# A graph layer that sums 140 quads of edges in its loop, and the 141st in a branch at the end

## The chip, the core and the metric

The kernel runs on one core of a Trainium2 chip. A core has five engines, each with an instruction queue of its own: TensorE (PE, matrix products; its weight loads are listed as PEld), VectorE (DVE), ScalarE (ACT), GpSimd (POOL) and SyncE (SP), which here only starts transfers. [...]a "q" behind an engine's name (POOLq, SPq) means its sequencer, which handles branches, register loads, semaphores and the starting of transfers. Transfers run on 16 DMA engines. The metric is the device time of one execution in microseconds (us).

## The reference

The input is a graph of 12,500 nodes with 128 features each and 400,000 edges sorted by their target `dst`. Each edge has a length (`edge_weight`). With the biases written out:

```python
rbf = exp(-(distances[:, None] - centers) ** 2 / (2.0 * width * width))       # 50 centers, 0 to 10
cut = 0.5 * (cos(pi * distances / CUTOFF) + 1.0) * (distances <= CUTOFF)      # CUTOFF = 10
W = (silu(rbf @ fw1 + fb1) @ fw2 + fb2) * cut[:, None]
messages = (h[src] @ pw + pb) * W
agg = segment_sum(messages, dst, num_segments=num_atoms)
y = h + (silu(agg @ mw1 + mb1) @ mw2 + mb2)
out = layernorm(x + y)                                                        # h is x
```

An edge whose length is over 10 adds nothing to `agg`. The lengths are spread evenly from 0 to 56.3, so most edges drop out; in the inputs of the reference 71,145 of the 400,000 stay.

## The kernel before, in words

**Packing.** The edges are read in 7 chunks, 128 rows of consecutive edges at a time. `pack` moves the edges that stay to the front of each row, and an indirect store writes them densely, one after the other, to `packed` in device memory. What follows works on that dense list. 512 places of the list are a *quad*, two quads (one pass of `basis`, `first`, `silu`) an *oct*. `QB` says at which quad each chunk's share begins; its last entry, 141, is the number of quads for which there is room, and `NQ = QB[-1]` that of the quads that the loop works on. 141 quads have 72,192 places.

**The loop over quads** (L1043) does for each quad `q`: `fetch` (L638, four indirect gathers on POOL, 128 rows of 512 bytes each, into one of four buffers `quad` from quad 32 on); `radials` (lengths of an oct, spread over 64 partitions, one transfer a quad on SP); `basis` (ACT), `first` (PE) and `silu` (ACT) for the radial filter; `second` (PE, L707 and L710); `message` (DVE, L717: filter times gathered rows); `place` (DVE, four operations at L726 that build a 128x128 matrix of places and weights each); `sum_up` (PE, L742); `base_of` (DVE's queue loads the target column into a register) and `add` (DVE, L765, two operations that add the sums to `aggT`). Gathers are issued several quads ahead. `added(q)` says up to which quad the adds are done when quad `q` begins: in pairs up to `NQ - 14`, one quad behind after that. The order on every engine is the order in which the program issues the instructions; a small model of time (`clock`, `pool`, `there_at`) decides only where steps of `pack` and the gathers are put.

**Node groups.** `aggT` holds the sums, features on partitions. A group is 512 nodes and is named by its first tile of 128 nodes: 0, 4, ..., 96 (the last has 212 nodes). Since the edges are sorted, the first groups are complete long before the last quad. `begin` (L888) computes from `added`, `done_to` and `NQ` during which four quads a group is worked on: `node_first` (PE, L776 and L777, then tanh on ACT, L779), `node_silu` (DVE, L786), `node_second` (PE, L274 and L277), `node_stats` (DVE, L801 and L805). Every four groups `scaled` computes the scales of the normalization in 18 small DVE operations (L814 to L829), and `normalize` (ACT, L844) with its store follows, one group a quad. With 141 quads, group 76 is worked on in quads 131 to 134, group 80 in 133 to 136, group 84 in 136 to 139, and group 88 begins in quad 139 (`node_first`) and quad 140 (`node_silu`): it is the list `last`. Groups 92 and 96 are in no quad.

**The end.** After the loop the last quad is added (L1093), and `finish` (L860) works on group 88 from `node_second` on and on groups 92 and 96 from the start, then normalizes them; the halves of that last step are on ACT (L844) and DVE (L841).

**The check of the counts.** The kernel takes for granted that the edges fit into the room and the windows that it gives them. When all chunks are packed, `count` (L926) sums what would speak against it into one number, `bad_i`, and every engine loads that number into a register (L1092). At the end a branch (L1099) that runs if it is over 0 computes everything again in a general way. That branch isn't taken with these inputs; each engine jumps over it.

Of the kernel before, what the change touches and what calls it, by code (L numbers as in the profile page):

```python
# [10 lines left out]
F32 = mybir.dt.float32  # L11
BF16 = mybir.dt.bfloat16
I32 = mybir.dt.int32
# [6 lines left out]
P = 128  # L20
# [10 lines left out]

ROWS = (180, 435, 500, 512, 512, 512, 474)
CAPS = (58, 124, 136, 136, 136, 136, 132)
QB = (0, 7, 26, 48, 70, 93, 115, 141)
NC_ = len(QB) - 1
WIDE_C = 4
NQ = QB[-1]
AHEAD = 3  # L40
AHEAD_X = 4
FROM_X = 8
# [15 lines left out]
def kernel(  # L58
# [39 lines left out]
    E = src.shape[0]  # L98
    R_MAX = max(ROWS)
    NT = -(-N // P)  # L100
    NP = 2 * NQ
    MW = 2 * (NQ * QE + QE)

    CLEAR = (0, 128 * P, 384 * P, MW)
    assert H == P == W and GOT == LATER[1] + 4 and LATER[0] % GOT == 0
# [131 lines left out]
    def sides():  # L237


        nc.vector.tensor_scalar(third, part_f, -1.0, 1.0 / 3, op0=OP.add, op1=OP.mult)  # L240
        for v in (1.5, -1.5):
            nc.vector.tensor_scalar(third, third, v * (1 << 23), None, op0=OP.add)
        nc.vector.scalar_tensor_tensor(side, third, -3.0, part_f, op0=OP.mult, op1=OP.add)
        nc.vector.tensor_scalar(side, side, float(MW), None, op0=OP.mult)


        nc.vector.tensor_scalar(end, part_f, 2.0, float(2 * NQ * QE), op0=OP.mult, op1=OP.add)

    k_f, rbf_scale, rbf_bias = (keep.tile([P, 1], F32, name=k)
                                for k in ("k_f", "rbf_scale", "rbf_bias"))  # L250
# [34 lines left out]
    cnt = keep.tile([P, NC_], F32, name="cnt")  # L285
    span = keep.tile([P, NC_], F32, name="span")
    run = keep.tile([P, 1], F32, name="run")
    bad_i = keep.tile([1, 1], I32, name="bad_i")
    late_f = keep.tile([P, NC_], F32, name="late_f")
    nc.vector.memset(late_f, 0.0)  # L290
    lim = keep.tile([64, NC_], F32, name="lim")
# [355 lines left out]

    def quads(o):

        return [q for q in (2 * o, 2 * o + 1) if q < NQ]  # L650

    def radial(o, lengths, eng=None):

# [103 lines left out]
    def added(q):  # L757

        return max((q - 2) // 2 * 2 if q < NQ - 14 else q - 1, 0)
# [165 lines left out]

    def count():  # L926

        miss = keep.tile([P, 5], F32, name="miss")
        nc.vector.tensor_reduce(miss[:, 0:1], cnt, AX.X, OP.add)
        nc.vector.tensor_reduce(miss[:, 1:2], took, AX.X, OP.add)  # L930
        nc.vector.tensor_add(miss[:, 0:1], miss[:, 0:1], miss[:, 1:2])
        nc.vector.tensor_reduce(miss[:, 1:2], span, AX.X, OP.max)
        nc.vector.tensor_scalar(miss[:, 1:2], miss[:, 1:2], 127.5, None, op0=OP.is_gt)
        nc.vector.tensor_reduce(miss[:, 2:3], late_f, AX.X, OP.min)
        nc.vector.tensor_scalar(miss[:, 2:3], miss[:, 2:3], 0.0, None, op0=OP.is_lt)
        nc.vector.tensor_reduce(miss[:, 3:4], low, AX.X, OP.min)
# [106 lines left out]
    for q in range(NQ):  # L1043
# [44 lines left out]
        if not todo and not counted:  # L1088
            counted.append(q)
            count()  # L1090
        elif counted and total is None:
            total = nc.values_load(bad_i[0:1, 0:1], min_val=0, max_val=2 * E)  # L1092
# [6 lines left out]
    with tc.If(total > 0):  # L1099
        nc.vector.memset(aggT, 0.0)  # L1100
        def again(e0, seen):

            def column(ap, dt, name):
                t = work.tile([P, QT], dt, name=name, bufs=1)
                nc.sync.dma_start(t, ap[ds(e0, QE)].rearrange("(j p) -> p j", p=P))
                return t

            idx = column(src, I32, "idx")
            loc_i = column(dst, I32, "loc_i")
            lengths = column(edge_weight, F32, "lengths")  # L1110
            loc = work.tile([P, QT], F32, name="loc", bufs=1)
            nc.vector.tensor_copy(loc, loc_i)
            wgt = work.tile([P, QT], F32, name="wgt", bufs=1)
            near = work.tile([P, QT], F32, name="near", bufs=1)
            nc.vector.tensor_scalar(near, lengths, CUTOFF, 0.5, op0=OP.is_le, op1=OP.mult)
            if seen:
                nc.vector.memset(near[:, :seen], 0.0)
            fold(wgt, lengths, work.tile([P, QT], F32, name="fold_f", bufs=1),
                 work.tile([P, QT], I32, name="fold_i", bufs=1))
            cosine(wgt)  # L1120
            nc.vector.scalar_tensor_tensor(wgt, wgt, 1.0, near, op0=OP.add, op1=OP.mult)
            fetch(-2, idx)
            radial(-1, [edge_weight[ds(e0, QE)].rearrange("(o e) -> o e", o=1)])
            basis(-1)
            first(-1)
            silu(-1)
            second(-2)
            u = own(0, "msg", 0)
            for j in range(QT):
                nc.vector.tensor_scalar(u[:, j, :], pu_of[-2][:, j * H:(j + 1) * H],  # L1130
                                        wgt[:, j:j + 1], None, op0=OP.mult)
            free.append(pu_of.pop(-2))
            msg = own(1, "msg", 0)
            nc.vector.tensor_mul(msg, u, got_of.pop(-2))
            for n0 in range(0, N, WS):
                n = min(WS, N - n0)
                at = work.tile([P, QT], F32, name="at")
                nc.vector.tensor_scalar(at, loc, float(-n0), None, op0=OP.add)
                pa = bank()
                for j in range(QT):  # L1140
                    hot = work.tile([P, WS], F32, name="hot_all", tag="d", bufs=3)
                    nc.vector.tensor_scalar(hot[:, :n], iota_n[:, :n], at[:, j:j + 1],
                                            None, op0=OP.is_equal)
                    nc.tensor.matmul(pa[:, :n], msg[:, j, :], hot[:, :n],
                                     start=(j == 0), stop=(j == QT - 1))
                nc.vector.tensor_add(aggT[:, n0:n0 + n], aggT[:, n0:n0 + n], pa[:, :n])
                free.append(pa)

        with tc.For_i(0, E // QE, 1) as g:
            again(g * QE, 0)  # L1150
        if E % QE:
            again(E - QE, QT - E % QE // P)
        finish(tiles)


# [24 lines left out]
```

## Time and profile before

| | |
|---|---|
| median of 3 runs | 816.37 us (815.54 to 817.31) |
| the profiled execution: its own time | 819.14 us |
| the profiled execution: span, first to last instruction | 817.3 us |
| mean granted TensorE clock | 0.851 |
| POOL busy | 569.8 us (70%) |
| PE busy | 604.2 us (74%) |
| DVE busy | 587.5 us (72%) |
| ACT busy | 381.1 us (47%) |

The span is what the trace holds; the execution's own time is measured around it and is 1.84 us longer. In lines of instructions the columns are: start and duration in us (timeline), engine, line of the program, operation, result and sources by the program's names with their shapes, how many instructions, and in brackets how long the engine stood idle before them and what ended that. In lines that begin with a line number the columns after the bar are busy time in us, mean duration in ns, and idle time with what ended most of it; or, in lines with two slashed triples, minimum, median and maximum duration in ns and the start of the first and the last. "issue" is idle time in which the profile shows nothing that was waited for.

### The profile page before, as it was taken

What the parts mean: (1) busy time and instruction counts of PE and PEld (TensorE: products, weight loads), DVE (VectorE), ACT (ScalarE), POOL (GpSimd) and SP (SyncE); (2) the same over time, 40 slices, a digit from 0 to 9 for tenths busy, and PEclk for the clock granted to TensorE, in tenths of its full rate; (3) what the DMA queues carried; (4) which work ended last, traced back from release to release, by engine and by line L of the source; (5) the groups of instructions that cost most, each with busy time, mean ns of one, the idle gap of its engine ahead of it and who ended that gap; (6) DMA issues with size and microseconds to landing.
All of it is one profiled execution on the core that took longest, in us unless ns stands there. A gap on an engine that the chain in (4) does not pass through costs nothing.

```text
span 817.3 us, 11550 instructions
## 1 busy us (share of the span) xinstructions
PE 604.2 (74%) x3492; PEld 475.7 (58%) x3492; DVE 587.5 (72%) x1785; ACT 381.1 (47%) x536; POOL 569.8 (70%) x585
## 2 busy tenths in 40 slices
PE   6777878768776777866588678887777887688661
PEld 5766657547664555655456556665555665566551
DVE  7962568989978877979796677657566565756764
ACT  6536656434644353253354254636444633454421
POOL 1375477777777777777777777777777777777730
PEclk9978899977987776778779788999889989889875
DMA  6968734342234223332531622723622642371221
GB/s 198 263 201 246 191 85 105 90 117 75 74 107 112 65 65 112 103 78 53 144 87 52 164 65 79 194 68 104 170 79 58 159 122 78 80 188 52 81 83 48
DMA packets 88189, 91.86 MB, mean 112 GB/s; under 512 B 13864, under 2 KB 67832, under 8 KB 88120
## 3 DMA queue, kind: packets, MB, share of 16 engines
q1 hardware_dynamic: 69320, 52.77, 22.6%
q0 software_dynamic: 18544, 38.17, 18.6%
q8 instruction: 29, 0.48, 0.2%
q14 instruction: 40, 0.33, 0.1%
q10 hardware_dynamic: 256, 0.11, 0.1%
HBM read 75.29 MB, written 15.71 MB: 111 GB/s over the span
## 4 chain that ended last, share of the span: by engine, by line
DVE 24%; POOL 20%; DMA 20%; issue 16%; PE 14%; ACT 3%; DVEq 2%; SPq 0%; POOLq 0%; ACTq 0%
POOL quad L643 20%; DMA quad<-proj,srci 18%; DVE hot L726 4%; PE sums L742 4%; PE bank L277 3%; DVE aggT L765 3%; DVE quad L726 2%; PE bank L710 2%; DVE msg L717 2%; DVEq L751 2%; PE ph L693 2%; DVE quad L717 1%; DVE r_d L438 1%; DVE nodes L429 1%; PE bank L595 1%
## 5 line engine op out<-in xcount | busy, mean ns | idle before, releaser
L643 POOL DMA_INDIRECT quad<-proj,srci x532 | 524.9, 987 | 169.6 <-issue 131.7
L710 PEld LDWEIGHTS bank<-fw_sb,s 128*128 128x128 f32 x1128 | 175.2, 222 | 37.1 <-issue 28.8
L710 PE MATMUL bank<-fw_sb,s 128*128 128x128 f32 x1128 | 173.5, 304 | 0.0
L699 ACT ACTIVATE s<-ph 128x1024 f32<-128x1024 f32 (+1 forms) x71 | 72.3, 1018 | 197.9 <-PE ph L693 197.8
L742 PEld LDWEIGHTS sums<-hot,msg 128*128 128x128 f32 x696 | 92.3, 206 | 115.4 <-DVE msg L717 84.8
L742 PE MATMUL sums<-hot,msg 128*128 128x128 f32 x696 | 109.3, 304 | 52.6 <-DVE msg L717 52.5
L742 PE MATMUL sums<-quad,quad 128*128 128x128 f32 x432 | 79.3, 342 | 67.8 <-DVE quad L717 67.6
L742 PEld LDWEIGHTS sums<-quad,quad 128*128 128x128 f32 x432 | 70.2, 247 | 74.3 <-DVE quad L717 74.3
L717 DVE TENSOR_TENSOR msg<-bank,quad 128x512 f32<-128x512 f32 x87 | 59.6, 685 | 71.9 <-DMA quad<-proj,srci 62.7
L726 DVE TENSOR_SCALAR hot<-iota_n,dl,cut 128x128 f32<-128x128 f32 x348 | 98.6, 358 | 12.7 <-PE sums L742 8.9
L693 PE MATMUL ph<-rbf,w_sb 51*128 51x512 f32 x282 | 89.5, 711 | 1.5 <-ACT s L699 1.4
L717 DVE TENSOR_TENSOR quad<-bank,quad 128x512 f32<-128x512 f32 x54 | 37.1, 688 | 56.1 <-DMA quad<-proj,srci 54.3
L765 DVE TENSOR_TENSOR aggT<-aggT,sums 128x128 f32 x212 | 60.4, 285 | 22.3 <-PE sums L742 10.9
L707 PE MATMUL bank<-fb_b,ones_b 96*128 96x512 bf16 x141 | 61.5, 436 | 19.3 <-DVE msg L717 8.7
L683 ACT ACTIVATE rbf<-d,rbf_bias,rbf_scale 128x512 f32<-128x512 f32 (+1 forms) x71 | 57.0, 803 | 37.9 <-DMA d<-near_d 37.7
L726 DVE TENSOR_SCALAR quad<-iota_n,dl,cut 128x128 f32<-128x128 f32 x216 | 61.8, 360 | 3.0 <-issue 0.7
L779 ACT ACTIVATE zt<-bank 128x512 f32<-128x512 f32 (+1 forms) x25 | 14.6, 583 | 81.5 <-PE bank L777 81.5
L844 ACT ACTIVATE x<-x,by,rs 128x128 f32<-128x128 f32 x91 | 37.1, 481 | 30.6 <-DVE by L814 30.6
L277 PEld LDWEIGHTS bank<-pw_sb,xT 128*128 128x128 f32 x260 | 40.0, 222 | 11.3 <-issue 5.1
L684 ACT ACT_TABLE_LOAD x36 | 46.2, 1283 | 0.6
L699 ACT ACT_TABLE_LOAD x36 | 46.2, 1283 | 0.6
L684 ACT ACTIVATE rbf<-rbf 128x512 f32<-128x512 f32 (+1 forms) x71 | 44.7, 630 | 1.5
(169 smaller groups left out, 744.2 us busy)
## 6 DMA issues: line engine op xcount, KB each, us to landing
d<-near_d SPq DMA_DIRECT2D x141, 128.0 KB
x<-in_x_dram SPq DMA_DIRECT2D x48, 256.0 KB
quad<-proj,srci POOLq DMA_INDIRECT x532, 2.6
proj<-hp SPq DMA_DIRECT2D x24, 256.0 KB
out_dram<-x SPq DMA_DIRECT2D x24, 256.0 KB
packed<-zero_i SPq DMA_DIRECT2D x6, 188.0 KB
pair<-packed SPq DMA_DIRECT2D x3, 264.0 KB
r_d<-in_edge_weight_dram SPq DMA_DIRECT2D x3, 256.0 KB
```

Source lines behind the costliest of these rows:

```text
L277: nc.tensor.matmul(to[:m, k, :], lT[:, k * P:k * P + m], w, start=False, stop=(k == a + c - 1))
L643: nc.gpsimd.indirect_dma_start(out=got[:, j, :], out_offset=None, in_=proj if table is None else table, in_offset=bass.IndirectOffsetOnAxi ...
L683: nc.scalar.activation(rbf[:u], d[:u], AF.Square, bias=rbf_bias[:u], scale=rbf_scale[:u])
L684: nc.scalar.activation(rbf[:u], rbf[:u], AF.Exp, scale=-1.0 / (2.0 * width * width))
L693: nc.tensor.matmul(ph[:, h, :], w1_sb[p0:p0 + KR], rbf[p0:p0 + KR], start=True, stop=True)
L699: nc.scalar.activation(s[:, :n], ph[:, :n], AF.Silu)
L707: nc.tensor.matmul(pu, ones_b[:, :P], bias_b["fb2"].rearrange("k j f -> k (j f)"), start=True, stop=False)
L710: nc.tensor.matmul(pu[:, j * H:(j + 1) * H], s[:, j * P:(j + 1) * P], fw2_sb, start=False, stop=(j == QT - 1))
L717: nc.vector.tensor_mul(msg, pu.rearrange("p (j f) -> p j f", j=QT), got_of.pop(q))
L726: nc.vector.tensor_scalar(hot[:, j, :], iota_n[:, :W], dl[:, at[0], at[1]], cut[:, at[0], at[1]], op0=OP.is_equal, op1=OP.mult)
L742: nc.tensor.matmul(pa[:, k * W:(k + 1) * W], msg[:, j, :], hot[:, j, :], start=(j % n == 0), stop=(j % n == n - 1))
L765: nc.vector.tensor_add(to, to, pa[:, k * W:(k + 1) * W])
```

## The change

`NQ` becomes 140, while the room for packed edges stays at 141 quads (`NP`, `MW` and the end of the packed list are now computed from `QB[-1]`). The loop so works on quads 0 to 139. Everything that is computed from `NQ` follows: `added` changes its rule at quad 126 instead of 127, group 76 is worked on in quads 130 to 133, groups 80 and 84 keep their quads, group 88 is in no quad any more and belongs to `finish` with 92 and 96, and the x rows of these three groups are loaded in quad 136.

`count` computes two more numbers: by how many the staying edges exceed 140 x 512 = 71,680 (0 if they don't), and the sum of that and the number from before. All three are loaded into registers on every engine. At the end an outer branch (`either > 0`) holds two inner ones: `more > 0` works on quad 140 and on groups 92 and 96 again, with the functions of the loop, and `total > 0` is the branch from before, unchanged. With 71,145 edges all three numbers are 0.

```diff
-NQ = QB[-1]
+NQ = QB[-1] - 1
...
-    NP = 2 * NQ
-    MW = 2 * (NQ * QE + QE)
+    NP = 2 * QB[-1]
+    MW = 2 * (QB[-1] * QE + QE)
...
-        nc.vector.tensor_scalar(end, part_f, 2.0, float(2 * NQ * QE), op0=OP.mult, op1=OP.add)
+        nc.vector.tensor_scalar(end, part_f, 2.0, float(2 * QB[-1] * QE), op0=OP.mult, op1=OP.add)
...
-    bad_i = keep.tile([1, 1], I32, name="bad_i")
+    bad_i = keep.tile([1, 3], I32, name="bad_i")
...
-        return [q for q in (2 * o, 2 * o + 1) if q < NQ]
+        return [q for q in (2 * o, 2 * o + 1) if q < QB[-1]]
...
-        miss = keep.tile([P, 5], F32, name="miss")
+        miss = keep.tile([P, 6], F32, name="miss")
         nc.vector.tensor_reduce(miss[:, 0:1], cnt, AX.X, OP.add)
+        nc.vector.tensor_copy(miss[:, 4:5], miss[:, 0:1])
...
-        nc.tensor.matmul(cp[:1, :4], ones[:, 0:1], miss[:, :4], start=True, stop=True)
-        nc.vector.tensor_reduce(miss[0:1, 4:5], cp[:1, :4], AX.X, OP.add)
+        nc.tensor.matmul(cp[:1, :5], ones[:, 0:1], miss[:, :5], start=True, stop=True)
+        nc.vector.tensor_reduce(miss[0:1, 5:6], cp[:1, :4], AX.X, OP.add)
+        nc.vector.tensor_copy(bad_i[:, 0:1], miss[0:1, 5:6])
+        nc.vector.tensor_scalar(miss[0:1, 5:6], cp[:1, 4:5], float(-NQ * QE), 0.0, op0=OP.add,
+                                op1=OP.max)
         free.append(cp)
-        nc.vector.tensor_copy(bad_i, miss[0:1, 4:5])
+        nc.vector.tensor_copy(bad_i[:, 1:2], miss[0:1, 5:6])
+        nc.vector.tensor_add(bad_i[:, 2:3], bad_i[:, 0:1], bad_i[:, 1:2])
...
             total = nc.values_load(bad_i[0:1, 0:1], min_val=0, max_val=2 * E)
+            more = nc.values_load(bad_i[0:1, 1:2], min_val=0, max_val=E)
+            either = nc.values_load(bad_i[0:1, 2:3], min_val=0, max_val=3 * E)
...
-    with tc.If(total > 0):
-        nc.vector.memset(aggT, 0.0)
+    with tc.If(either > 0):
+
+        with tc.If(more > 0):
+            o = NQ // 2
+            fetch(NQ)
+            radial(o, [near_d[2 * NQ:2 * NQ + 2].rearrange("(o p) e -> o (p e)", o=1)])
+            basis(o)
+            first(o)
+            silu(o)
+            second(NQ)
+            place(NQ)
+            sum_up(NQ, message(NQ))
+            base_of(NQ)
+            add(NQ)
+            finish([t0 for t0 in tiles if (t0 + 4) * P > done_to(2 * NQ)])
+
+
+        with tc.If(total > 0):
+            nc.vector.memset(aggT, 0.0)
...
```

More of the change, by code (lines that the diff above doesn't have):

```diff
@@ L1096 @@
     finish([t0 for t0 in tiles if t0 not in begin], last)
-    with tc.If(total > 0):
-        nc.vector.memset(aggT, 0.0)
[L1101 to L1139, printed above, removed]
-                for j in range(QT):
[L1141 to L1153, printed above, removed]
@@ new lines, with again, column @@
+    with tc.If(either > 0):
[14 more added lines that the diff above has]
+            nc.vector.memset(aggT, 0.0)
+            def again(e0, seen):
+                def column(ap, dt, name):
+                    t = work.tile([P, QT], dt, name=name, bufs=1)
+                    nc.sync.dma_start(t, ap[ds(e0, QE)].rearrange("(j p) -> p j", p=P))
+                    return t
+                idx = column(src, I32, "idx")
+                loc_i = column(dst, I32, "loc_i")
+                lengths = column(edge_weight, F32, "lengths")
+                loc = work.tile([P, QT], F32, name="loc", bufs=1)
+                nc.vector.tensor_copy(loc, loc_i)
+                wgt = work.tile([P, QT], F32, name="wgt", bufs=1)
+                near = work.tile([P, QT], F32, name="near", bufs=1)
+                nc.vector.tensor_scalar(near, lengths, CUTOFF, 0.5, op0=OP.is_le, op1=OP.mult)
+                if seen:
+                    nc.vector.memset(near[:, :seen], 0.0)
+                fold(wgt, lengths, work.tile([P, QT], F32, name="fold_f", bufs=1),
+                     work.tile([P, QT], I32, name="fold_i", bufs=1))
+                cosine(wgt)
+                nc.vector.scalar_tensor_tensor(wgt, wgt, 1.0, near, op0=OP.add, op1=OP.mult)
+                fetch(-2, idx)
+                radial(-1, [edge_weight[ds(e0, QE)].rearrange("(o e) -> o e", o=1)])
+                basis(-1)
+                first(-1)
+                silu(-1)
+                second(-2)
+                u = own(0, "msg", 0)
+                for j in range(QT):
+                    nc.vector.tensor_scalar(u[:, j, :], pu_of[-2][:, j * H:(j + 1) * H],
+                                            wgt[:, j:j + 1], None, op0=OP.mult)
+                free.append(pu_of.pop(-2))
+                msg = own(1, "msg", 0)
+                nc.vector.tensor_mul(msg, u, got_of.pop(-2))
+                for n0 in range(0, N, WS):
+                    n = min(WS, N - n0)
+                    at = work.tile([P, QT], F32, name="at")
+                    nc.vector.tensor_scalar(at, loc, float(-n0), None, op0=OP.add)
+                    pa = bank()
+                    for j in range(QT):
+                        hot = work.tile([P, WS], F32, name="hot_all", tag="d", bufs=3)
+                        nc.vector.tensor_scalar(hot[:, :n], iota_n[:, :n], at[:, j:j + 1],
+                                                None, op0=OP.is_equal)
+                        nc.tensor.matmul(pa[:, :n], msg[:, j, :], hot[:, :n],
+                                         start=(j == 0), stop=(j == QT - 1))
+                    nc.vector.tensor_add(aggT[:, n0:n0 + n], aggT[:, n0:n0 + n], pa[:, :n])
+                    free.append(pa)
+            with tc.For_i(0, E // QE, 1) as g:
+                again(g * QE, 0)
+            if E % QE:
+                again(E - QE, QT - E % QE // P)
+            finish(tiles)
```

## The prediction

> **What bounds the kernel now.** I read the page first, then the order of time on POOL, then the last 40 us on all engines, then the releasers of the final branch. The costliest group is POOL's gathers, four for each quad of 512 edges:
>
> ```profile
> L643 POOL DMA_INDIRECT quad<-proj,srci x532 | 524.9, 987 | 169.6 <-issue 131.7
> L1092 POOLq TENSOR_LOAD <-bad_i x1: 505/505/505, 501.7 to 501.7; - x1
> L1099 POOLq COMPARE_BRANCH  x1: 54/54/54, 777.1 to 777.1; - x1
> L1099 SPq COMPARE_BRANCH  x1: 53/53/53, 812.2 to 812.2; - x1
> L1099 SPq EVENT_SEMAPHORE  x8: 17/17/17, 815.1 to 815.6; - x8
> ```
>
> From 91.2 us to 785.5 us POOL runs one gather after the other: 0.94 us and 0.30 us of "issue", so 1.25 us each and 5.0 us a quad. Everything else in the loop has slack against that. A saved quad is therefore worth 5.0 us at most, and only if the tail follows POOL. Lines of the timeline (start, duration) show that it does not quite:
>
> ```profile
> 779.57 0.94 POOL L643 DMA_INDIRECT quad<-proj,srci  x1 [0.31 <-issue]
> ...
> 784.57 0.94 POOL L643 DMA_INDIRECT quad<-proj,srci  x1 [0.30 <-issue]
> ...
> 785.23 0.69 DVE L717 TENSOR_TENSOR quad<-bank,quad 128x512 f32<-128x512 f32 x1
> ...
> 785.97 2.08 PE L742 MATMUL sums<-quad,quad 128*128 128x128 f32 x8 [4.41 <-DVE quad L717]
> 788.09 0.61 DVE L765 TENSOR_TENSOR aggT<-aggT,sums 128x128 f32 x2 [1.14 <-PE sums L742]
> 788.61 0.68 DVE L786 SCALAR_TENSOR_TENSOR zs<-zt,bank 128x512 f32<-128x512 f32 x1
> 789.21 0.68 DVE L717 TENSOR_TENSOR msg<-bank,quad 128x512 f32<-128x512 f32 x1
> ...
> 789.95 2.08 PE L742 MATMUL sums<-hot,msg 128*128 128x128 f32 x8 [1.90 <-DVE msg L717]
> ...
> 792.06 0.61 DVE L765 TENSOR_TENSOR aggT<-aggT,sums 128x128 f32 x2 [1.65 <-PE sums L742]
> ...
> 792.72 2.07 PE L777 MATMUL bank<-aggT,mw_sb 128*128 128x512 f32 x2 [0.28 <-DVE aggT L765]
> ...
> 794.77 0.95 PE L777 MATMUL bank<-aggT,mw_sb 128*128 128x212 f32 x2
> ...
> 795.93 1.20 PE L277 MATMUL bank<-mw_h,zs 128*128 128x128 f32 x8
> ...
> 797.17 0.69 DVE L801 SCALAR_TENSOR_TENSOR x<-x,bank 128x512 f32<-128x512 f32 x1 [4.39 <-PE bank L277]
> ```
>
> The message of quad 139 (785.23) and of quad 140 (789.21) start 3.0 and 2.0 us after their edges landed: the last gather of each starts at 779.57 and 784.57, and a gather lands 2.6 us (median) after its start. DVE was busy with the statistics of node group 84: 18 small operations from 781.70 to 785.22. After quad 140's add (792.06) come the exposed products of the last groups, to 797.17. What follows that (groups 92 and 96, normalization, stores, end) takes 817.3 - 797.17 = 20.1 us.
>
> **The sum is made against the span 817.3 us** of the profiled execution, whose own time is 819.14; the median of the runs is 816.37. The difference in us goes over to the median.
>
> **Removed: quad 140.** Off POOL 4 x 1.25 = 5.0 us; off DVE message 0.69, place 1.11, adds 0.61; off PE the product of `first` 1.12, `second` 1.43, `sum_up` 2.08; off ACT two table loads of 1.28, 0.80, 0.63 and 0.60; off SP one 128 KB read. On the path is only what stands between quad 139's first add and the last add: 788.09 to 792.67, 4.58 us.
>
> **What is the last quad then?** Quad 139 is limited by DVE. From message(138) at 777.94 to message(139) at 785.23 DVE never idles (message, place, adds, statistics): 7.29 us, and the change leaves these operations as they are. Message(138) itself could start at 774.56 + 2.6 + 0.1 = 777.25; it was 0.7 late from a backlog that began with the 16-column statistics of groups 64 to 76 at 757 to 762. Group 76 moves one quad earlier (`added` changes its rule at 126 instead of 127), so these statistics fall between quads 132 and 133, and the backlog has one more quad to drain. I start message(139) at 777.25 + 7.29 = 784.55 (bounds 784.55 and 785.23).
>
> **Added to the tail: node group 88** starts in `finish` instead of in quads 139 and 140. From 784.55: message to end of `sum_up` 2.82 as before, 787.37; four adds in a row, 1.20, plus one register read of 0.31 that is partly covered, taken 1.35, end 788.77. PE then does 88's product (2.07), 92's bias and product (0.42 and 2.07), 96's (0.93), the bias and the eight products of `node_second` (0.2 and 1.9): 7.6 us, if all at the slow clock. The tanh (0.60) and `zs` (0.68) of group 88 lie beside 92's and 96's products; without that cover they cost 1.3 us. Also moved: the x load of group 88 from quad 134 to 136, behind one store more on SP and still some 20 us ahead of its use, and normalizations 80 and 84 (ACT, 1.65 each, with their stores) into `finish`. ACT is idle there (11.3 us before the last normalization), and the stores lie before 809.
>
> **The clock decides the size.** Row: L777 takes 2.07 at 792.72, and L277's eight products run at the fast rate from about 796.1, so 3.4 us of unbroken work raised the clock. By that row PE turns fast at 788.8 + 3.4 = 792.2; 4.2 us of the 7.6 are left and take 2.1; `node_second` ends at 794.3 and the path gains 797.13 - 794.3 = 2.8. [...]
>
> **Added in the middle: `count` and two register loads.** Four more DVE operations of 0.2 us at 498 delay DVE by 0.8 us. A message may be about 11 us late before POOL lacks a buffer (four buffers; three quads of 5.0 lie between, less the landing): nothing. Two more loads on each engine, 0.31 to 0.51 us each, and on SP two register operations more with each. On POOL gathers are queued behind them, on PE the products of the next `second`, on ACT a normalization, on DVE the next `zs`, on SP the stores. POOL's sequencer runs ahead: it was past its last gather and at the final branch at 777.1, when the last gather began only at 784.57. That is 7.5 us of cover against 1.0 us of loads: 0 taken, 1.0 if the cover is gone.
>
> **Added at the end: a longer body to jump over.** [...]Row: SP branches at 812.2 and does its next work at 815.1, 2.85 us. [...] I take 0.
>
> **Sum:** 817.3 - 2.0 = 815.3 for the span, and 816.37 - 2.0 = 814.4 us for the median (-0.24%).
>
> **Rivals.** [...] (b) POOL's 5.0 us come through whole, 811.4: for it, POOL paces the loop; against it, the 18 operations on DVE do not move. The 2.8 above and a fast clock also in 92's `node_second` (1.89 at 799.40) give 812.7. (c) Slower: the final jump of SP waits for instructions twice more, at the target and at the end block, 2 x 2.85 = 5.7, 820.1. It decides from 3.6 us on (2.0 + 1.6). For it: 2.85 us are there already, and PE's branch took 3.4 us; against it: in the trace of before one wait serves both blocks. (d) The change doesn't do what it says: the count is over 71,680 and the branch runs; the inputs exclude it.
>
> **How the numbers follow.** Main case 0.55 (812.8 to 815.3), (a) 0.28, (b) 0.09, (c) 0.08. Within 0.2% of the median, 1.6 us, is about what a measurement tells from no change: the border is 814.74. Main case: 0.46 below it, 0.09 above; (a) within, but for 0.01; (b) faster, (c) slower. That makes faster 0.55, same 0.36, slower 0.09. The range 812.3 to 816.7 leaves out half of (b), all of (c) and the worst of (a), 0.15 together.
>
> **What would show it.** POOL's last gather ends near 780.5 with no gap near 501; the statistics of group 76 lie before message(133); message(139) starts between 784.5 and 785.3; the last adds end near 788.8; the first `x` of `finish` starts between 794.3 and 796.4; from there to the end 20.1 us. Wrong: a gap on POOL after the register loads, message(139) after 786, more than 2.9 us between SP's branch and its next event, or any matmul of quad 140.

## The result, and the profile after

| | kernel before | changed kernel |
|---|---|---|
| median, first measurement (6 executions each) | 816.93 us (815.54 to 817.99) | 812.97 us (811.21 to 816.24) |
| ratio, first measurement | | 0.9958 (95%: 0.9942 to 0.9975) |
| median, second measurement | 815.66 us (23 executions) | 815.84 us (12 executions) |
| ratio, second measurement | | 1.0003 (95%: 0.9982 to 1.0025) |
| profiled execution: own time | 819.14 us | 812.78 us |
| profiled execution: span | 817.3 us | 810.8 us |

The first measurement shows a gain of 3.4 us by the ratio (4.0 by the medians) where 2.0 was forecast. The second shows none: its interval reaches from 1.5 us faster to 2.0 us slower. Here and below, a ratio uses only the executions within 1.5% of the fastest of their kernel.

From the page after, the summary of its chain of waits (shares of the span) and its row of gathers:

```profile
DVE 26%; DMA 18%; POOL 17%; PE 17%; issue 16%; ACT 3%; DVEq 2%; SPq 0%; POOLq 0%; ACTq 0%
L644 POOL DMA_INDIRECT quad<-proj,srci x528 | 519.9, 985 | 168.7 <-issue 132.6
```

Four gathers fewer, 985 ns each as before (987). The register loads and the final branch in the view by line (engine, operation, duration in ns, start in us):

```profile
L1098 POOLq TENSOR_LOAD <-bad_i x1: 511/511/511, 499.0 to 499.0; - x1
L1099 POOLq TENSOR_LOAD <-bad_i x1: 293/293/293, 499.6 to 499.6; - x1
L1100 POOLq TENSOR_LOAD <-bad_i x1: 292/292/292, 499.9 to 499.9; - x1
L1106 POOLq COMPARE_BRANCH  x1: 54/54/54, 769.9 to 769.9; - x1
L1106 SPq COMPARE_BRANCH  x1: 53/53/53, 806.2 to 806.2; - x1
L1106 SPq EVENT_SEMAPHORE  x8: 17/17/17, 808.6 to 809.1; - x8
```

POOL's sequencer made three loads between 499.0 and 500.2. The timeline shows what POOL itself did at that time:

```profile
498.93 0.95 POOL L644 DMA_INDIRECT quad<-proj,srci  x1 [0.30 <-issue]
500.18 0.95 POOL L644 DMA_INDIRECT quad<-proj,srci  x1 [0.30 <-DVE v L821]
501.44 0.94 POOL L644 DMA_INDIRECT quad<-proj,srci  x1 [0.30 <-issue]
```

The gathers stay 1.25 us apart: the loads cost POOL nothing. SP goes from its branch to the next event in 2.4 us (2.85 before): the longer body to jump over costs nothing either. The end of the loop and the last part, in the timeline:

```profile
774.29 0.69 DVE L718 TENSOR_TENSOR quad<-bank,quad 128x512 f32<-128x512 f32 x1 [1.74 <-DMA quad<-proj,srci]
...
776.44 0.68 DVE L802 SCALAR_TENSOR_TENSOR x<-x,bank 128x512 f32<-128x512 f32 x1
...
776.65 0.94 POOL L644 DMA_INDIRECT quad<-proj,srci  x1 [0.30 <-issue]
...
781.42 0.69 DVE L718 TENSOR_TENSOR quad<-bank,quad 128x512 f32<-128x512 f32 x1
782.17 2.07 PE L743 MATMUL sums<-quad,quad 128*128 128x128 f32 x8 [5.65 <-DVE quad L718]
784.28 0.61 DVE L766 TENSOR_TENSOR aggT<-aggT,sums 128x128 f32 x2 [2.17 <-PE sums L743]
785.50 0.61 DVE L766 TENSOR_TENSOR aggT<-aggT,sums 128x128 f32 x2 [0.61 <-DVE aggT L766]
786.17 2.08 PE L778 MATMUL bank<-aggT,mw_sb 128*128 128x512 f32 x2 [1.50 <-DVE aggT L766]
788.46 1.48 PE L778 MATMUL bank<-aggT,mw_sb 128*128 128x512 f32 x2
789.87 0.54 PE L778 MATMUL bank<-aggT,mw_sb 128*128 128x212 f32 x2
790.47 1.05 PE L278 MATMUL bank<-mw_h,zs 128*128 128x128 f32 x8
791.56 0.69 DVE L802 SCALAR_TENSOR_TENSOR x<-x,bank 128x512 f32<-128x512 f32 x1 [1.96 <-PE bank L278]
793.79 1.16 PE L278 MATMUL bank<-mw_h,zs 128*128 128x128 f32 x8 [2.06 <-DVE zs L787]
```

Message(138) (774.29) now begins when its edges have landed (the bracket says so); message(139) (781.42) still waits for DVE's own work. After the last sums two pairs of adds follow with 0.61 us between them, then the products of groups 88, 92 and 96, of which the first is slow (2.08), the second changes its rate (1.48) and the others are fast. From the last gather of quad 139 (776.65) to the end at 810.8 are 34.15 us. In the profile before, the last gather of quad 139 is at 779.57 and the end at 817.3: 37.73 us. So 3.58 of the 6.5 us between the spans lie here. The other 2.9 us were there already when that gather began; the change has no work that would explain them.

### The profile page after: what moved, and what is told of

It reads as the page before. It is cut to its first block, busy times and chain, and to the rows that moved or that the text cites. A ratio compares the mean times of both kernels' runs of the same rounds, so it can differ in the third digit from the quotient of the medians.

```text
span 810.8 us, 11505 instructions
## 1 busy us (share of the span) xinstructions
PE 595.8 (73%) x3473; PEld 468.9 (58%) x3473; DVE 586.8 (72%) x1782; ACT 376.6 (46%) x531; POOL 564.7 (70%) x581
## 4 chain that ended last, share of the span: by engine, by line
DVE 26%; DMA 18%; POOL 17%; PE 17%; issue 16%; ACT 3%; DVEq 2%; SPq 0%; POOLq 0%; ACTq 0%
POOL quad L644 17%; DMA quad<-proj,srci 16%; PE sums L743 5%; DVE hot L727 4%; PE bank L278 3%; PE bank L711 3%; DVE msg L718 3%; DVE aggT L766 2%; PE ph L694 2%; DVE quad L727 2%; DVEq L752 2%; DVE r_d L439 2%; DVE nodes L430 1%; DVE quad L718 1%; DVE st L806 1%
## 5 line engine op out<-in xcount | busy, mean ns | idle before, releaser
L644 POOL DMA_INDIRECT quad<-proj,srci x528 | 519.9, 985 | 168.7 <-issue 132.6
L711 PEld LDWEIGHTS bank<-fw_sb,s 128*128 128x128 f32 x1120 | 172.8, 220 | 36.3 <-issue 28.4
L711 PE MATMUL bank<-fw_sb,s 128*128 128x128 f32 x1120 | 171.2, 303 | 0.0
L700 ACT ACTIVATE s<-ph 128x1024 f32<-128x1024 f32 x70 | 71.7, 1024 | 199.2 <-PE ph L694 199.1
L743 PEld LDWEIGHTS sums<-hot,msg 128*128 128x128 f32 x688 | 95.2, 214 | 117.4 <-DVE msg L718 86.5
L743 PE MATMUL sums<-hot,msg 128*128 128x128 f32 x688 | 112.5, 313 | 55.1 <-DVE msg L718 55.0
L743 PE MATMUL sums<-quad,quad 128*128 128x128 f32 x432 | 76.0, 332 | 61.9 <-DVE quad L718 61.9
L743 PEld LDWEIGHTS sums<-quad,quad 128*128 128x128 f32 x432 | 67.4, 237 | 67.6 <-DVE quad L718 67.6
L718 DVE TENSOR_TENSOR quad<-bank,quad 128x512 f32<-128x512 f32 x54 | 37.1, 687 | 55.1 <-DMA quad<-proj,srci 52.4
L684 ACT ACTIVATE rbf<-d,rbf_bias,rbf_scale 128x512 f32<-128x512 f32 x70 | 56.2, 803 | 35.8 <-DMA d<-near_d 35.7
L845 ACT ACTIVATE x<-x,by,rs 128x128 f32<-128x128 f32 x91 | 36.9, 481 | 20.3 <-DVE by L815 20.3
L685 ACT ACTIVATE rbf<-rbf 128x512 f32<-128x512 f32 x70 | 44.1, 630 | 1.5
```

The lines of the kernel that those rows point to most:

```text
L644: nc.gpsimd.indirect_dma_start(out=got[:, j, :], out_offset=None, in_=proj if table is None else table, in_offset=bass.IndirectOffsetOnAxi ...
L684: nc.scalar.activation(rbf[:u], d[:u], AF.Square, bias=rbf_bias[:u], scale=rbf_scale[:u])
L685: nc.scalar.activation(rbf[:u], rbf[:u], AF.Exp, scale=-1.0 / (2.0 * width * width))
L700: nc.scalar.activation(s[:, :n], ph[:, :n], AF.Silu)
L711: nc.tensor.matmul(pu[:, j * H:(j + 1) * H], s[:, j * P:(j + 1) * P], fw2_sb, start=False, stop=(j == QT - 1))
L718: nc.vector.tensor_mul(msg, pu.rearrange("p (j f) -> p j f", j=QT), got_of.pop(q))
```

## Experiments

The theory under test: the gain is what the section from message(139) to the end says it is, message(139) is held by DVE, the products of the last part are slow for the clock alone, and what the change adds elsewhere is free. The rivals are named with each run.

The runs e1 to e4 and f1 to f6 were made on two chips where every kernel took 225 to 245 us longer (the kernel before: median 1059.51 and 1043.58 us) and executions of one kernel lay up to 37 us apart. Their ratios can tell little below 0.5%, but the last part of their traces, from the `x` of group 84 on, runs without the long waits that lie ahead of it, and can be read. The runs g0 to g2 and h0 were made on two others, as quick as that of the first measurement.

A measure that is free of the loop's length is needed to compare these traces: the time from the `x` operation of group 84 (776.44 above, the last before the statistics of groups 80 and 84) to the end of the span. The clock columns are the granted TensorE clock from message(139) to the first `x` of the last part, and from there to the second; the last column is the eight products of group 92.

| run | x(84) to end, us | clock to the first `x`, to the second | products of group 92, us |
|---|---|---|---|
| kernel before | 37.2 | 0.57, 0.79 | 1.89 |
| kernel before, again (h0) | 37.1 | 0.57, 0.81 | 1.82 |
| changed kernel | 34.4 | 0.61, 1.00 | 1.16 |
| changed kernel, again (g0) | 34.3 | 0.61, 1.00 | 1.16 |
| the same instructions (g1) | 34.9 | 0.57, 1.00 | 1.16 |
| 140 quads alone (e1) | 36.0 | 0.56, 0.74 | 2.08 |
| 140 quads alone (f1) | 36.5 | 0.55, 0.77 | 2.05 |
| 141 quads, group 88 left to the last part (e2) | 36.8 | 0.58, 1.00 | 1.16 |
| idle products that end too early (e4) | 36.3 | 0.55, 0.79 | 1.90 |
| scales after the adds (e3) | 32.8 | 0.55, 0.76 | 2.07 |
| scales after the adds (f3) | 31.8 | 0.67, 0.82 | 1.79 |
| group 88's product in quad 139 (f6) | 34.1 | 0.52, 0.90 | 1.44 |
| TensorE kept busy (f4) | 32.3 | 1.00, 0.85 | 1.64 |
| all together (g2) | 29.9 | 0.77, 1.00 | 1.16 |

**140 quads alone** (twice). The changed kernel without what was added for the branch; the check of `total` and its branch stay as before.

```diff
-    bad_i = keep.tile([1, 3], I32, name="bad_i")
+    bad_i = keep.tile([1, 1], I32, name="bad_i")
...
-            more = nc.values_load(bad_i[0:1, 1:2], min_val=0, max_val=E)
-            either = nc.values_load(bad_i[0:1, 2:3], min_val=0, max_val=3 * E)
...
-    with tc.If(either > 0):
-        with tc.If(more > 0):
...
+    with tc.If(total > 0):
```

> The loop works on 140 quads as in the changed kernel, but the count, its two further numbers, the two further register loads and the branch for quad 140 are left out (only the branch from before stands at the end). My theory: the loads lie under the gathers that POOL has queued and the jump costs the same, so the ratio to the kernel before is that of the changed kernel, 0.9958 within 0.001, and on POOL the gathers near 498 us stand 1.25 us apart in both. Rival (the added loads or the longer body cost what they last, about 0.9 us and more): 0.9945 or less.

> The loop of 140 quads without the further sums of count, the two register loads and the outer branch (this version leaves out the branch for quad 140). [...] Rival: loads and longer jump cost part of the quad that was saved; then this version is faster, 0.9945 or less.

Measured 0.9882 (0.9824 to 0.9940, 6 executions) and 0.9968 (0.9925 to 1.0012, 12 executions) of the kernel before. Against the theory, the changed kernel's 0.9958 within 0.001, the first lies wholly on the rival's side (0.9945 or less); the second holds both. On these chips that is no verdict either way, and that the additions are free rests on the traces: the gathers above, and SP's branch, which takes 2.6 and 2.9 us to its next event without the outer branch and 2.3 to 2.4 with it. And with the same order of work behind message(139), the last part is slower here than in the changed kernel's first profile. The timeline of the second run:

```profile
1001.13 1.91 PE L777 MATMUL bank<-aggT,mw_sb 128*128 128x512 f32 x2
...
1003.01 0.95 PE L777 MATMUL bank<-aggT,mw_sb 128*128 128x212 f32 x2
...
1007.50 2.05 PE L277 MATMUL bank<-mw_h,zs 128*128 128x128 f32 x8 [2.06 <-DVE zs L786]
```

The same products as above took 1.48, 0.54 and 1.16 there, and take 1.91, 0.95 and 2.05 here. TensorE turned fast later, and after 2.06 us of waiting for `zs` it was slow again, which it was not there. The busy times by stretch show the granted clock (third number from the right; ahead of it the length and the busy us of PE, PEld, DVE, ACT and POOL). The same run:

```profile
1000.00:1004.10 4.10, 4.10 (x9) 1.86 (x7) 0.69 (x1) 1.25 (x3) 0.00 (x0) 0.50 0.01 2
1004.20:1007.50 3.30, 1.25 (x10) 0.86 (x8) 2.15 (x6) 3.27 (x9) 0.00 (x0) 1.00 0.20 61
1007.70:1011.00 3.30, 1.96 (x9) 1.59 (x9) 1.38 (x5) 0.00 (x0) 0.00 (x0) 0.50 0.27 80
```

And the changed kernel:

```profile
789.40:796.20 6.80, 3.56 (x24) 2.50 (x22) 3.52 (x11) 3.90 (x10) 0.00 (x0) 1.00 0.26 77
796.20:799.00 2.80, 1.36 (x5) 0.98 (x5) 1.34 (x7) 0.00 (x0) 0.00 (x0) 0.50 0.03 6
```

The full clock is held for 3.4 us in one and for 6.8 in the other. The two traces of the first measurement list the granted clock by stretches, 72 in the kernel before and 62 in the changed kernel: in each trace all the changes lie on one grid of 3.413 us, to within 0.002 us. So in these traces the clock moved in whole steps of 3.4 us. Where the steps lie against the program differs: the product of group 88 starts 0.2 us into a step in the changed kernel and, by the clocks granted around it (to 0.1 us), 0.2 us in g0, 2.5 us in g1, 1.9 and 1.5 in e1 and f1.

How long PE worked in a step went with the clock of the next one. Counted over these two traces by the profile's busy times: of 53 steps at half clock with PE busy for less than 80% none was followed by the full clock, of 73 with 90% or more 62 were; of 56 steps at full clock with less than 40% none was followed by another, of 239 with 60% or more 237 were. In the changed kernel the step that began at 785.95 held 3.20 us of work, and the clock rose at 789.37, 3.2 us after the first of the products (786.17); the next held 2.37 us and the clock stayed for another. In f1 it rose at 1004.15, 5.3 us after the first product (998.84); 1.36 us of work were left for that step, and the clock was gone before the products of group 92. Which of the two these executions met went with where the steps fell. By the first table it is worth 1.6 to 2.2 us (36.0 and 36.5 against 34.3 and 34.4), all but some 0.2 us of it between message(139) and the second `x`.

**Group 88 left to the last part in the kernel before.** Edit: `if at_q + 3 > NQ: break` instead of `+ 2`, still 141 quads.

> The kernel before, 141 quads, with the one edit that node group 88 is not begun in quads 139 and 140 but belongs to the last step with groups 92 and 96. My theory: 0.6 us are won (its zs is not ahead of the last message any more) and 1.4 to 2.5 us are lost to its product and bias on PE after the last adds: ratio 1.001 to 1.0025, and the first x of the last step starts 0.8 to 1.9 us later against the last gather. Rival (its work hides in the last step too, so that the move is free): ratio 0.999 to 1.0005.

0.995 (0.9911 to 0.9989): below what either expectation allowed, so the time decides nothing. In the trace, from the start of the last adds (1035.89) to the first `x` (1042.13) are 6.24 us against 5.11 in the kernel before: 1.1 us for the move, within what the theory expected (0.8 to 1.9, there counted from the last gather, which on this chip is long done). TensorE then stayed fast through group 92 (1.16), which gave 0.7 us back.

**Scales after the adds** (twice). The changed kernel; the 18 statistics operations of groups 80 and 84 move behind the last adds.

```diff
-                if k % 4 == 3 or k + 1 == len(early):
+                if k % 4 == 3:
...
     for q in range(added(NQ), NQ):
         base_of(q)
         add(q)
+    if len(early) % 4:
+        scaled(early[len(early) // 4 * 4:], st_of[0])
```

> The changed kernel, with the 18 small operations that compute the scales of groups 80 and 84 moved from quad 139 to behind the last adds. My theory: message(139) waits for these operations and not for its rows, so it starts as soon as its rows land, 2.6 us after the start of the last gather instead of 4.8, and the time falls by about 2.0 us more: ratio about 0.993 (0.992 to 0.9945). Rival (POOL's last gather and its landing set the end, DVE follows): ratio as the changed kernel, 0.9958 within 0.001.

> The changed kernel with the 18 statistics operations of groups 80 and 84 behind the last adds instead of ahead of message(139). My theory: message(139) is held up by DVE's work and not by its edges, so it starts at their landing, 2.6 us after the last gather instead of 4.8, and the end comes about 2.2 us earlier, less some tenths for a colder clock: 0.9930 to 0.9942 of the kernel before. Rival: normalizations 80 and 84 and their stores, moved behind the adds, set the end instead, or PE's clock takes the gain: 0.9958 with 0.001 either way.

1.0013 (0.9955 to 1.0072) and 0.9913 (0.9876 to 0.9951): in time the first holds the rival and lies above all that the theory expected; the second holds the theory and touches the rival's edge (0.9948). The trace of the second:

```profile
994.06 0.68 DVE L802 SCALAR_TENSOR_TENSOR x<-x,bank 128x512 f32<-128x512 f32 x1
995.56 0.67 DVE L718 TENSOR_TENSOR quad<-bank,quad 128x512 f32<-128x512 f32 x1
996.29 1.16 PE L743 MATMUL sums<-quad,quad 128*128 128x128 f32 x8 [2.48 <-DVE quad L718]
```

Message(139) starts 1.50 us after x(84) instead of 4.98, and nothing else had to change for it: DVE takes up its operations in the program's order here, and its work ahead of the message, not the edges, held it. The whole of the last part is 4.7 us shorter than in the 140 quads alone on the same chip (36.5 to 31.8) and 3.3 in the other pair (36.0 to 32.8); the earlier start is worth 3.5, and the clock differs too: sums(139) took 1.16 us here and 2.08 in the other. On these chips the edges had landed long before; with POOL as the pace only 2.2 us can come through, which the last run of this section shows.

**Group 88's product in quad 139.** The changed kernel with `if at_q + 1 > NQ: break` and, in `finish`, `if k == 0 and t0 in z_of`.

> The changed kernel with the bias and product of group 88 in quad 139, ahead of the last sums, instead of in the final part. My theory: the product of 2.1 us lies in the path of the last part now, and it fills PE's idle time ahead of sums(139) when it is moved, so the end comes 1.0 to 2.1 us earlier: 0.9932 to 0.9946 of the kernel before. Rival: the product only kept PE busy while the clock rose, so that what follows runs slower by as much: 0.9958 with 0.001 either way.

0.996 (0.9904 to 1.0016): inconclusive in time. The product ran at 998.22 in 1.12 us, in time that PE had idle ahead of sums(139); in its place 92's product became the slow first one behind the adds (2.08). The last part is 2.4 us shorter than the 140 quads alone on the same chip, and 0.2 us shorter than the changed kernel's with its better clock, so of the 2.1 us only what the clock leaves is gained: between the theory and the rival.

**TensorE kept busy** (twice). The changed kernel with products that nothing reads (a row of ones by itself): 14 of them in quad 139 at first, then 24 in quad 139 and 5 ahead of the last adds.

```diff
+    def idle_products(n):
+        b = bank()
+        for _ in range(n):
+            nc.tensor.matmul(b, ones_b[:, :P], ones_b, start=True, stop=True)
+        free.append(b)
...
+        if q == NQ - 1:
+            idle_products(24)
...
+    idle_products(5)
     for q in range(added(NQ), NQ):
```

> The changed kernel, with 14 products of ones (512 columns each, result not used) on PE in quad 139, where PE stands idle for 5.7 us before the sums of that quad. My theory: the clock stays up, the sums of quad 139 take 1.1 instead of 2.07 us, the product of group 88 1.1 instead of 2.08, that of group 92 1.05 instead of 1.48: 1.0 to 2.4 us less than the changed kernel, ratio 0.993 to 0.9948. Rival (the clock of the end is set by other work, or the end waits for DVE): ratio 0.9958 within 0.001.

> The changed kernel with 24 idle products of 512 columns on PE in quad 139, ahead of sums(139), and 5 more between these and the product of group 88. My theory: the products of the last part are slow for the clock alone, so with PE kept busy sums(139) takes 1.1 us instead of 2.07, 88's product 1.1 instead of 2.08 and 92's 1.05 instead of 1.48, and the end comes 1.5 to 2.4 us earlier: 0.9928 to 0.9940 of the kernel before. Rival: the first products are slow for other reasons, or the idle ones push sums(139) back by as much as they save: 0.9958 with 0.001 either way, or more.

The first, 0.9958 (0.992 to 0.9996), missed its mark: the 14 products ended 2.96 us before sums(139), which still took 2.07 us. The second reached it; its time, 0.9903 (0.9858 to 0.9949), holds the theory and touches the rival's edge (timeline; L904 is the idle product):

```profile
1005.96 5.34 PE L904 MATMUL bank<-ones_b 96*128 96x512 bf16 x24
1012.11 1.16 PE L743 MATMUL sums<-quad,quad 128*128 128x128 f32 x8 [0.81 <-DVE quad L718]
...
1015.19 1.13 PE L778 MATMUL bank<-aggT,mw_sb 128*128 128x512 f32 x2 [0.63 <-DVE aggT L766]
...
1016.37 1.02 PE L778 MATMUL bank<-aggT,mw_sb 128*128 128x512 f32 x2
...
1017.33 0.54 PE L778 MATMUL bank<-aggT,mw_sb 128*128 128x212 f32 x2
1017.92 1.05 PE L278 MATMUL bank<-mw_h,zs 128*128 128x128 f32 x8
```

With 0.81 us of idle time instead of 5 or 6 ahead of it, sums(139) takes 1.16 instead of 2.07, and every product behind it its fast time. From message(139) to the first `x` are 7.65 us instead of 10.14 in the changed kernel. The products of the last part are slow for the clock alone; a full 2.5 us lie in it. Group 92's products, which wait 2.05 us again without such filling, fell back to 1.64.

**The changed kernel again**, unedited.

> The changed kernel once more, beside the next two. My theory: 0.9958 of the kernel before, as measured, with 0.002 either way; the part from the last gather of quad 139 to the end takes 34 to 36 us, and the loop ahead of it starts as early or as late as it happens, since the 2.9 us by which it ran ahead in the changed kernel's profile are no work of the change. Rival: those 2.9 us belong to the change, so POOL's first gather of the loop comes some 2 us earlier than in the kernel before in this profile too.

1.0003 (0.9982 to 1.0025), against 0.9958 expected with 0.002 either way: a miss, the measured interval lies wholly above that. The profiled execution has a span of 810.8 us, as the first had, and its parts are those of the first: 33.99 us from the last gather of quad 139 to the end (34.15), first gather of the loop at 88.88 us (90.25; before 91.19), 687.9 us from there to the last gather of quad 139 (686.4; before 688.4). But its own time, 812.80 us, is the shortest of this run's 12, whose median is 815.84; of the kernel before, 23 executions on this chip lay between 810.60 and 819.15 us. The rival's sign, a first gather some 2 us earlier, is in this profile (88.88 against 91.19); but the kernel before itself had it at 89.63 when it was profiled again (h0), so the two kernels' first gathers overlap.

**Register loads first.** The changed kernel with two loops, one of `base_of` and one of `add`, in place of one.

> The changed kernel with the register loads of the last two quads ahead of both pairs of adds. My theory: two loads of 0.30 us stand between the pairs now, so the 0.61 us of idle time between them go and the last add ends 1.2 us after the first starts instead of 1.8: 0.5 us off the end, a ratio 0.0006 below that of the changed kernel. Rival: the second pair waits for the first one's result whatever is loaded, the 0.61 us stay, and so does the time.

0.9991 (0.9971 to 1.0011). The 0.61 us between the pairs of adds stayed, and so did the two loads between them:

```profile
L752 DVEq TENSOR_LOAD <-base_i x2: 300/300/300, 784.5 to 784.9; - x2
```

The edit moved nothing. `added(140)` is 139, so only quad 139 is left to that loop, and the first of the two pairs is quad 138's, issued in the loop's last turn ahead of these loads. Up to the final branch this program issues the changed kernel's instructions in the same order, so it is a third profile of that order: from the last gather of quad 139 to the end 34.6 us; median 814.54. Whether the second pair waits for the loads or for the first pair wasn't tried.

**The kernel before again**, on a further chip.

> The kernel before, unchanged, against itself, with a profile of its own. Both theories say 1.000 with 0.0015 either way for the time; the profile tells them apart. Theory: what the change gains behind the last gather of quad 139 is real, so that part takes 37 to 38 us here, as in the first profile of the kernel before (37.7), against 34.0 to 34.6 in three profiles of the changed kernel and its variant; what differs between the two measurements lies in the loop. Rival: the first profile of the kernel before fell on a late rise of the clock, and that part takes 35 to 36.5 us here, so that the change is worth 1 to 2 us there and no more.

1.0009 (0.9991 to 1.0027) against itself. Its last gather of quad 139 and its last part in the timeline:

```profile
777.79 1.00 POOL L643 DMA_INDIRECT quad<-proj,srci  x1 [0.30 <-issue]
...
783.72 0.69 DVE L717 TENSOR_TENSOR quad<-bank,quad 128x512 f32<-128x512 f32 x1
...
791.15 2.07 PE L777 MATMUL bank<-aggT,mw_sb 128*128 128x512 f32 x2 [0.27 <-DVE aggT L765]
...
795.68 0.69 DVE L801 SCALAR_TENSOR_TENSOR x<-x,bank 128x512 f32<-128x512 f32 x1 [4.47 <-PE bank L277]
```

From 777.79 to the end of the span at 815.5 are 37.71 us; the first profile had 37.73. Three profiles of the changed order on the quick chips show 34.15, 33.99 and 34.60, that is 3.1 to 3.7 us less. This is what the theory said, but the rival does not fall with it, because both profiles met the clock's steps at nearly the same place, and a late one. In the first profile, step by step:

```profile
789.39:792.81 3.42, 2.59 (x10) 1.90 (x10) 1.67 (x6) 0.00 (x0) 0.00 (x0) 0.50 0.01 2
792.81:796.22 3.41, 3.41 (x8) 1.88 (x9) 0.00 (x0) 1.02 (x3) 0.00 (x0) 0.50 0.00 0
```

PE's last burst begins there with the sums of quad 140 (789.95), 0.6 us into a step. After that step, with 2.59 us of work, the clock stayed at 0.50, and the full clock came at 796.22, 6.3 us after the burst began. In h0, by the shares of the clock in the table (0.57 and 0.81), the burst (788.37) began 0.4 us into a step that held 2.75 us of work, and the clock came after 6.4 us. In the changed kernel a burst that began 0.2 us into a step, with 3.20 us of work in it, had the clock after 3.2 us. How long the kernel before takes when its steps fall otherwise no profile shows, so an unknown part of the 3.1 to 3.7 us is the place of the steps.

**All together**: scales after the adds, group 88's product in quad 139 and its `zs` ahead of the last adds, the register loads ahead of that, and idle products ahead of the adds (5) and ahead of the products of groups 92 and 96 (7 each). The end of the edit:

```diff
...
     for q in range(added(NQ), NQ):
         base_of(q)
+    idle_products(5)
+    for t0 in last:
+        node_silu(t0)
+    for q in range(added(NQ), NQ):
         add(q)
+    if len(early) % 4:
+        scaled(early[len(early) // 4 * 4:], st_of[0])
-    finish([t0 for t0 in tiles if t0 not in begin], last)
+    finish([t0 for t0 in tiles if t0 not in begin], last, warm=True)
...
+            if warm and k:
+                idle_products(7)
             node_second(t0)
```

> The changed kernel with the statistics of groups 80 and 84 behind the last adds, the product of group 88 in quad 139 and its zs ahead of the adds, the register loads first, and idle products on PE where it would wait for the adds (5) and for the zs of groups 92 and 96 (7 each). My theory: message(139) 2.2 us earlier, from it to the first x of the final part some 6.8 us instead of 10.1, and 0.4 us less in the products of group 96; 5.9 us off the end, 0.9872 to 0.9905 of the kernel before. Rival: the parts hide one another, since statistics behind the adds hold up the first x on DVE and idle products push the real ones back: no more than 2 us off, 0.993 or more.

808.85 us median, 0.992 (0.9893 to 0.9947) of the kernel before, on the chip where the changed kernel stood at 1.0003. It beats both, and by 7.0 us the changed kernel's median there. The ratio to the kernel before misses the 0.9872 to 0.9905 expected, which was reckoned from 0.9958, and its interval still holds the rival's 0.993; but the rival allowed 2 us off the end, and the timeline shows more:

```profile
776.18 0.94 POOL L644 DMA_INDIRECT quad<-proj,srci  x1 [0.30 <-issue]
778.78 0.69 DVE L718 TENSOR_TENSOR quad<-bank,quad 128x512 f32<-128x512 f32 x1 [1.20 <-DMA quad<-proj,srci]
779.53 2.08 PE L743 MATMUL sums<-quad,quad 128*128 128x128 f32 x8 [1.32 <-DVE quad L718]
781.64 0.61 DVE L766 TENSOR_TENSOR aggT<-aggT,sums 128x128 f32 x2 [2.17 <-PE sums L743]
...
783.36 0.60 DVE L766 TENSOR_TENSOR aggT<-aggT,sums 128x128 f32 x2
...
785.67 1.05 PE L278 MATMUL bank<-mw_h,zs 128*128 128x128 f32 x8
...
787.26 0.63 DVE L802 SCALAR_TENSOR_TENSOR x<-x,bank 128x512 f32<-128x512 f32 x1
```

Message(139) now starts 2.60 us after the last gather, when its edges have landed, instead of 4.77. The first `x` follows 8.48 us after it instead of 10.14, held up at its end by the statistics on DVE (to 787.2; the products were done at 786.7). The last part, from the last gather, is 29.7 us against 34.0 to 34.6: 4.3 to 4.9 us, of 5.9 expected.

## Why the prediction was right, and where its sizes were off

The first measurement (812.97 us) lies inside the forecast range and on its faster side; the second is what the forecast called no difference. The mechanism held step by step, with sizes off in both directions. That the first measurement fell inside the range is in part luck: it shows 3.4 to 4.0 us where 2.0 were forecast, and the second, of the same two programs, shows none.

- **POOL, register loads, jump: as forecast.** No gap among the gathers near 500 us, POOL's branch at 769.9 with six gathers still to start, 2.3 to 2.4 us for SP's jump against the 2.85 that were taken as unchanged.
- **Backlog: as forecast.** The statistics of group 76 lie between messages 132 and 133 (748.1 to 751.7), and message(138) begins 2.5 to 2.6 us after the last gather of its quad in all three profiles, against 3.4 and 3.5 before.
- **Message(139): as forecast.** 4.69 to 4.77 us after the last gather where 4.98 was reckoned, 5.66 and 5.93 before. The scales of groups 80 and 84, moved behind the adds, show that DVE held it.
- **Four adds, taken as 1.35 us: 1.83 measured.** "One register read that is partly covered" were two of 0.30 us, with 0.61 us of idle time between the pairs. Besides, quad 138's pair need not have been there: its sums were done near 776.5, but it is issued behind quad 139's sums, which share a tile with quad 138's (L738), and its wait is for those (2.17 us). That the shared tile is the cause is read from the code and wasn't tried; the trace before agrees, where the adds at 788.09 (quad 138's, not quad 139's as the prediction has it) wait for sums(139), while quad 139's at 789.81 start before sums(140) at 789.95.
- **The clock: it rose, in two of three profiles earlier than reckoned.** No run shows the 2.0 us that the sum takes off: the 2.8 us beside its row at 792.72 were the author's reading of one trace, and 2.0 an estimate that allowed for a later rise. From the last add to the first `x` the 2.0 us stand for 6.4 us and the 2.8 for 5.6; measured 5.45, 5.46 and 6.02 in the three profiles of the changed order on the quick chips, 6.3 and 6.5 in e1 and f1. From 88's product to the full clock it took 3.2 us in two of these profiles, the shortest rise here, with 3.20 us of work in the step before it in the changed kernel; 4.4 in the third and 4.9 and 5.3 in e1 and f1. The row itself was a misreading: its 3.4 us count from the product at 792.72; PE had worked since 789.95 with 0.28 us of idle time, and the clock came 6.3 us after that, near the latest that these traces show (6.4). So the span of the kernel before, from which the 2.0 us were taken, was itself a late case.
- **"What follows takes 20.1 us" was the step that failed.** It took 19.2 us in the three profiles: node_second of 92 ran at 1.16 instead of 1.89, since the clock that had risen held for a second step. It took 20.1 and 20.3 in e1 and f1, where it didn't. In these traces it went with the work that was left for the step in which the clock had risen: 2.37 us in the changed kernel, where it held, 1.36 in the kernel before, 1.49 and 1.36 in e1 and f1. With three groups' products behind the adds instead of two it can be more, which the main case put at nothing. That a high clock would last over the 2 us of waiting was put into rival (b) only.

With these terms the last part gains 0.6 to 2.9 us, as the clock has it (x(84) to end, 37.1 to 37.2 before, 34.3 to 36.5 after), and 0.7 to 0.9 us more from the earlier message(138): 1.3 to 3.8 us in all, around the 2.0 that were forecast, against the two profiles of the kernel before.

Rival (a), 0.28 by the forecast, where group 88 eats the gain because the clock stays low and message(139) comes no earlier, came near in e1 and f1. Rival (b)'s 811.4 us needed POOL's 5.0 us whole and is excluded by message(139); its fast clock at group 92 was seen. Rivals (c) and (d) fall: no second wait at the jump, and no matmul of quad 140. That SP waits for instructions there, as (c) has it, is the author's reading; the profile before lists three packets (0.02 MB) of the queue that it calls instruction in that wait of 2.85 us.

**What stays open.** The profiles differ by more than the last part does: the first by 2.9 us that lie ahead of the last gather of quad 139. The first gather of the loop began at 88.9 to 90.3 us in the profiles of the changed order and at 89.6 and 91.2 in those before, and the way from there to the last gather of quad 139 took 686.4 to 687.9 against 688.2 and 688.4. These are five executions, and no step of the change explains them; executions of one kernel on one of the quick chips lie up to 9 us apart. So the 3.4 us of the first measurement can't be divided surely between the last part and this scatter, nor can the missing gain of the second be placed: the slower executions there have no trace. That they had the colder clock of e1 and f1 would account for up to 2 us, and that executions of the kernel before met better steps than its two profiles would take off more; both are only argued. Taking 24 executions of the changed order there together, the mean is 815.03 us against 815.37, a gain of 0.3 us with a standard error of 0.6.

## What to carry to other kernels

When the pacing engine loses a step at the end of a loop, the gain is what the chain behind it lets through: find what the last result waits for (here DVE's statistics, not the gathers), and move that first. In these traces a short burst of products after a wait ran at the clock that it met (the same eight products took 1.16 or 2.05 us), and the clock moved in steps of 3.4 us whose place against the program differed; reckon such work at both clocks, and where it stands on the path, fill the wait ahead of it (2.5 us from message(139) to the first `x` here). A gain of 0.3% needs both kernels on several chips: two measurements with narrow intervals gave 0.9958 and 1.0003.

## What was not expected of the hardware

Two chips ran the same programs in some 1,040 to 1,060 us. The summary of the chain of waits in the page of f1, beside the one above:

```profile
PE 21%; another core or an unknown queue 19%; issue 19%; DVE 18%; POOL 11%; ACT 6%; DMA 3%; DVEq 1%; SPq 0%; POOLq 0%; ACTq 0%
L643 POOL DMA_INDIRECT quad<-proj,srci x528 | 520.3, 985 | 337.5 <-issue 146.8
```

POOL was as quick per gather (985 ns) but idle twice as long (337.5 us for 168.7), and a fifth of the chain waits for something that the profile can't name. One such place in the timeline of that run:

```profile
918.48 1.06 PE L742 MATMUL sums<-quad,quad 128*128 128x128 f32 x8
...
926.97 0.61 DVE L765 TENSOR_TENSOR aggT<-aggT,sums 128x128 f32 x2 [8.46 <-remote]
```

The sums were done at 919.5 and DVE had nothing else to do, yet the add began at 926.97. Such waits, some 70 of them in this run and up to 23 us long, stand at a dozen lines of DVE and ACT, and in none of the profiles of the quicker chips. Their cause wasn't pursued.

A second surprise is smaller: of the changed kernel's three register loads in a row (near 500 us) the second and third took 0.27 to 0.31 us on every engine, where the first took 0.47 to 0.51 on all but DVE (0.31).
